# Attention scores of two heads on the two row halves of TensorE

## The chip, the cores and the metric

The kernel runs on one core of a Trainium2 chip. The metric is the device time of one execution in microseconds (us): the lower the better. The core has a matmul engine (TensorE, PE in the profile; its weight loads are a row of their own, PEld), a vector engine (DVE), an engine for activations (ACT), GpSimd (POOL) and SyncE (SP), which issues transfers. Each works through its own queue in order, and they wait for each other by semaphores. A matmul holds one operand, the weights, in the 128 x 128 array, and streams the other through it; the results land in PSUM, a memory of eight banks that hold 512 fp32 values in each of 128 partitions.

## The reference

One layer of a transformer: attention, then a mixture of experts, each between two norms. Cut to what matters:

```
x = x + LN(attention(LN(x)))          # x: 8 images of 256 rows, 256 wide
x = x + LN(experts(LN(x)))            # 8 experts, 2 chosen per row, and 2 shared ones

attention: q = rope(x Wq)             # 32 heads of 8
           k = rope(x Wk), v = x Wv   # 8 key heads of 8: four query heads share one
           scores = q k^T / sqrt(8)   # causal
           ctx = softmax(scores) v
           return ctx Wo + b
```

The whole is fp32. The attention has eight key heads, and for each of them four query heads, over 256 rows of each image.

## The kernel before

The kernel goes through the eight images (b = 0 to 7) in two row halves each (tt, 128 rows), and records every step with a due time by `at(when, step, ...)`; the steps are then issued sorted by these times, each onto all the engines it uses. So the due times alone, in units of one image, set the order in every queue: scores of one image are made beside the projections of the next and the shared experts of an earlier one. After the eight images come the routed experts (in blocks of 256 rows), the additions to the result and the last norm.

Scores in fp32 quality come from fp32r matmuls, which stream one column per step but keep fewer bits. So each head's eight values are split (`split`, POOL, and DVE for the first image's second half) into a rounded part and the rest; 32 rows hold the four combinations of both parts of q and k. Three key heads with 32 rows each, 96 rows (`SHIFT`), are one group; the eight heads make groups of three, three and two (`J`, `NS`, `heads_in`).

- `keysT` (L410) transposes the keys of a half by matmuls with an identity, three of them, 96, 96 and 64 columns of weights, and ACT or DVE copies the result to `kA`. `keys_apart` (L428) then moves it by three DMAs of SP into `kst`: one block of 256 columns per key head, in which only the 32 rows of that head are not zero. Thus a matmul over all 96 rows, whose other operand holds three heads, gives the scores of one head.
- `queriesT` (L437) transposes the queries: per half three groups of four matmuls, 96, 96 and 64 weight columns, each group copied by ACT to `qA` (L444).
- `maxima` (L468, L475, L482) computes scores with queries as weights, and up to 512 columns of several key heads. A second matmul (bf16, an identity as weights) adds the causal mask to the diagonal part, and DVE reduces to the negated maximum of each row. An image has 32 of these scores, each with its mask, in 26 banks.
- `split_shift` and `shiftT` (L500) split these maxima, transpose them and put them by three DMAs of SP into six further rows of `qA` (96 to 101). The same rows of `kst` hold ones for the head's own two of them (`place1`, `set_ones`), so that the next matmul subtracts the maximum.
- `weights_of` (L520, L528, L530) computes the scores again, transposed, over all 102 rows: one matmul of 512 columns for each key head and pair of row blocks. ACT makes the exp, and POOL clears the part above the diagonal.
- `values` (L548) multiplies four of these with the values: four matmuls on four strips of 32 columns of the array at once. `softmaxed` (L568) turns and divides.

All the scores, the shared experts' products (`gu`, `po`) and later the experts share five PSUM banks (`ps_mm`); transposes have two of their own (`ps_tp`). Operands that live longer are held three times over (`qAs`, `ksts`, by b % 3); they are cleared at their first use by `clear_operands`, on DVE for the first, on POOL for the others.

Of the kernel before, what the change touches and what calls it, by code (L numbers as in the profile page):

```python
# [9 lines left out]
F32 = mybir.dt.float32  # L10
# [8 lines left out]
P = 128  # L19
EPS = 1e-5  # L20
NEG = -1e30
HD = 8
HB = 32
SHIFT = 96
# [4 lines left out]
def attn_moe_kernel(  # L29
# [63 lines left out]
    J = 3  # L93
    NS = -(-NKV // J)
    KR = SHIFT + 2 * J
# [74 lines left out]

    place1 = aconst.tile([P, J, 1], F32, name="place1")
    nc.gpsimd.memset(place1[SHIFT:P], 1.0)
    for sign, base in ((1, 0), (-1, 1)):
        nc.gpsimd.affine_select(
            out=place1[SHIFT:P],
            in_=place1[SHIFT:P],
            pattern=[[-2 * sign, J], [0, 1]],
            compare_op=ALU.is_ge,
            fill=0.0,
            base=base,  # L180
            channel_multiplier=sign,
        )
    qAs, ksts, v_aug = {}, {}, {}

    def clear_operands(i):
        qAs[i] = aconst.tile([P, NS * G, T], F32R, name=f"qA_{i}")
        engine = nc.gpsimd if i > 0 else nc.vector
        engine.memset(qAs[i][:, (NS - 1) * G :, :].bitcast(F32), 0.0)
        t = ksts[i] = aconst.tile([P, NKV, T], F32R, name=f"kst_{i}")
        engine.memset(t[0:SHIFT].bitcast(F32), 0.0)  # L190

    def set_ones(i):
        t = ksts[i]
        for k0 in range(0, NKV, J):
            n = min(J, NKV - k0)
            nc.scalar.copy(
                t[SHIFT:P, k0 : k0 + n, :], place1[SHIFT:P, 0:n, :].to_broadcast([P - SHIFT, n, T])
            )
# [139 lines left out]
    def project(b, tt):  # L338
# [32 lines left out]
        qs = work.tile([P, NS * G, J * HB], F32R, tag="qs", name=f"qs{b}_{tt}")  # L371
        ks = work.tile([P, NKV * HB], F32R, tag="ks", name=f"ks{b}_{tt}")
        held["qs", b, tt] = full, qs, ks

    def split(b, tt, i):

        full, qs, ks = held["qs", b, tt]
        if i == 0:
            to = ks.rearrange("p (h b a d) -> p h b a d", b=2, a=2, d=HD)
            of = full[:, NH:, :].unsqueeze(2).to_broadcast([P, NKV, 2, HD])  # L380
            pairs = [(to[:, :, :, 0, :], to[:, :, :, 1, :], of)]
        else:
            c, b2 = divmod(i - 1, 2)
            n = heads_in(c)
            to = qs[:, ts(c, G), 0 : n * HB].rearrange(
                "p g (j a b d) -> p j g a b d", a=2, b=2, d=HD
            )
            of = full[:, c * J * G : (c * J + n) * G, :].rearrange(
                "p (j g) d -> p j g d", g=G
            )  # L390
            pairs = [(to[:, :, :, 0, b2, :], to[:, :, :, 1, b2, :], of)]
# [5 lines left out]
    def heads_in(c):  # L397
        return min(J, NKV - c * J)

    def keysT(b, tt):  # L400
        ks = held["qs", b, tt][2]
        if tt == 0:
            held["kA", b] = work.tile(
                [SHIFT, NS, T], F32R, tag="kA", name=f"kA{b}", bufs=1
            )
        kA = held["kA", b]
        pt = ps_tp.tile([P, NS, P], F32, tag="tp", name=f"pkT{b}_{tt}")
        for c in range(NS):
            n = heads_in(c) * HB
            nc.tensor.matmul(  # L410
                pt[0:n, c, :],
                lhsT=ks[:, c * SHIFT : c * SHIFT + n],
# [4 lines left out]
        whole = NKV // J  # L417
        copied = copier(b - 1)
        copied(kA[:, 0:whole, ts(tt, P)], pt[0:SHIFT, 0:whole, :])
        if whole < NS:  # L420
            copied(kA[0:n, whole, ts(tt, P)], pt[0:n, whole, :])

    def keys_apart(b):
        kA, kst = held.pop(("kA", b)), ksts[b % 3]
        for j in range(J):
            n = len(range(j, NKV, J))
            part = slice(HB * j, HB * j + HB)
            nc.sync.dma_start(  # L428
                out=kst[part, j:NKV:J, :].bitcast(F32), in_=kA[part, 0:n, :].bitcast(F32)
            )  # L430

    def queriesT(b, tt, c):
        qs = held["qs", b, tt][1]
        n = heads_in(c) * HB
        pt = ps_tp.tile([P, G, P], F32, tag="tp", name=f"pqT{b}_{tt}_{c}")
        for g in range(G):
            nc.tensor.matmul(  # L437
                pt[0:n, g, :],
                lhsT=qs[:, c * G + g, 0:n],
                rhs=ident_r,  # L440
                start=True,
                stop=True,
            )
        nc.scalar.copy(qAs[b % 3][0:n, ts(c, G), ts(tt, P)], pt[0:n])  # L444

    def maxima_of(b, tt):

        width = (tt + 1) * P
        for c in range(NS):
            per = min(512 // width, heads_in(c))  # L450
            for k0 in range(0, heads_in(c), per):
                nk = min(per, heads_in(c) - k0)
                ng = 512 // (nk * width)
                for g0 in range(0, G, ng):
                    yield c, c * J + k0, nk, g0, ng

    def maxima(b, tt, c, k0, nk, g0, ng):

        qA, kst = qAs[b % 3], ksts[b % 3]
        if ("nmx", b, tt) not in held:  # L460
            held["nmx", b, tt] = small.tile(
                [P, NKV, G], F32, tag="nmx", name=f"nmx{b}_{tt}", bufs=2
# [3 lines left out]
        sc = ps_mm.tile([P, ng, nk, width], F32, tag="mm", name="sc")  # L466
        for g in range(ng):
            nc.tensor.matmul(  # L468
                sc[:, g, :, :],
                lhsT=qA[0:SHIFT, c * G + g0 + g, ts(tt, P)],  # L470
# [835 lines left out]
```

## Time and profile before

| What | us |
|---|---|
| median of 6 runs (832.1 to 840.11) | 835.98 |
| the profiled execution | 841.12 |
| its span | 839.4 |
| PE busy, of the span | 774.6 (92%) |
| PEld busy | 589.7 (70%) |
| DVE busy | 421.7 (50%) |
| POOL busy | 344.5 (41%) |
| ACT busy | 259.9 (31%) |
| scores for the weights (L520), 192 matmuls | 97.2 |
| scores for the maxima (L468), 256 matmuls | 101.2 |
| mask (L475), 256 matmuls | 74.5 |
| values (L548), 384 rows of the profile | 58.2 |

A plain fp32 matmul stands as two rows in the profile, each of two passes; an fp32r, a bf16 one and a transpose stand as one. [...] A shape such as 96*128 means 96 rows and 128 weight columns. The tables' times count from the start of the span. The images take from about 20 us to about 515 us, and the routed experts the rest.

### The profile page before, as it was taken

Reading aid. Unit: us, or ns where it says so; the run is one execution under the profiler, and the core shown is the slowest. Engines: PE = TensorE matmul, PEld = TensorE weight load, DVE = VectorE, ACT = ScalarE, POOL = GpSimd, SP = SyncE. Lnnn points to the kernel's source line nnn. Section 1 sums busy time; section 2 is a strip of 40 time slices with the busy share of each in tenths; the row PEclk is TensorE's granted clock in tenths of the full one; section 3 lists DMA queues with packets and bytes.
Section 4 is the critical chain, followed back from the end, with each engine's and each line's share of the span. In section 5 each row is a group of like instructions: output and inputs, shape, how many; then the busy total and the mean of one; then the engine's idle time right before and its main releaser. Section 6 shows DMA issues by size and latency. Waiting matters only on the chain. (4 is left out here: it accounts for less than half of the span.)

```text
span 839.4 us, 11794 instructions
## 1 busy us (share of the span) xinstructions
PE 774.6 (92%) x4041; PEld 589.7 (70%) x4041; DVE 421.7 (50%) x1172; ACT 259.9 (31%) x567; POOL 344.5 (41%) x616
## 2 busy tenths in 40 slices
PE   5989899999999999999999987999999999999753
PEld 3545466767767767767756666888888888889742
DVE  5756677677677677676685446122222222222215
ACT  3554444234244234244234321112121111212103
POOL 4567445435435435434244422531213434252213
PEclk8799899999999999999999997999999999999986
DMA  5023300000000000000000005525556575779642
GB/s 151 6 83 87 87 16 16 7 21 15 7 22 15 7 22 16 13 15 15 21 8 2 27 0 201 184 55 196 156 164 211 146 226 149 212 201 338 223 114 100
DMA packets 31906, 74.62 MB, mean 89 GB/s; under 512 B 9136, under 2 KB 26032, under 8 KB 28896
## 3 DMA queue, kind: packets, MB, share of 16 engines
q1 hardware_dynamic: 20304, 58.17, 19.7%
q0 software_dynamic: 8224, 10.03, 7.1%
q10 hardware_dynamic: 3312, 5.60, 2.4%
q8 instruction: 35, 0.57, 0.3%
q14 instruction: 31, 0.25, 0.1%
HBM read 59.36 MB, written 11.80 MB: 85 GB/s over the span
## 5 line engine op out<-in xcount | busy, mean ns | idle before, releaser
L776 PE MATMUL gu<-xgT,w 128*128 128x256 f32 (+1 forms) x840 | 163.9, 354 | 0.6 <-issue 0.3
L776 PE MATMUL gu<-x2T,ws_sb 128*128 128x256 f32 x640 | 155.9, 391 | 5.2 <-PEq L1207 5.0
L776 PEld LDWEIGHTS gu<-xgT,w 128*128 128x128 f32 x840 | 144.4, 190 | 17.6 <-issue 0.5
L528 ACT ACTIVATE ex<-scT 128x512 f32<-128x512 f32 x192 | 113.6, 597 | 137.1 <-PE scT L520 124.8
L482 DVE TENSOR_REDUCE nmx<-sc 128x2 f32<-128x512 f32 (+2 forms) x208 | 129.2, 642 | 26.5 <-PE sc L475 26.2
L776 PEld LDWEIGHTS gu<-x2T,ws_sb 128*128 128x128 f32 x640 | 121.8, 196 | 27.5 <-issue 6.2
L530 POOL TENSOR_SCALAR_AFFINE_SELECT ex<-ex 128x512 f32<-128x512 f32 x128 | 81.1, 639 | 114.0 <-ACT ex L528 113.8
L979 DVE TENSOR_TENSOR act<-sg,gu 128x256 f32<-128x256 f32 (+1 forms) x105 | 40.9, 389 | 128.8 <-ACT sg L978 128.8
L468 PE MATMUL sc<-kst,qA 96*128 96x512 f32 (+2 forms) x256 | 101.2, 426 | 0.8 <-issue 0.5
L987 POOL DMA_INDIRECT sums<-yb,of x37 | 58.3, 1575 | 101.8 <-DVE yb L986 62.7
L520 PE MATMUL scT<-qA,kst 102*128 102x512 f32 x192 | 97.2, 514 | 1.8 <-DMA qA<-nm 1.8
L978 ACT ACTIVATE sg<-gu 128x256 f32<-128x256 f32 (+1 forms) x105 | 37.6, 358 | 190.1 <-PE gu L776 190.1
L789 PE MATMUL po<-ws_sb,sact 128*128 128x256 f32 x320 | 78.3, 403 | 13.8 <-DVE sact L806 9.5
L789 PEld LDWEIGHTS po<-ws_sb,sact 128*128 128x128 f32 x320 | 63.8, 203 | 28.8 <-DVE sact L806 9.9
L789 PE MATMUL po<-w,act 128*128 128x256 f32 x370 | 83.2, 379 | 0.0
L789 PEld LDWEIGHTS po<-w,act 128*128 128x128 f32 x370 | 68.8, 190 | 8.5
L475 PE MATMUL sc<-mask,ident_b 128*128 128x256 bf16 (+2 forms) x256 | 74.5, 294 | 0.0
L924 POOL DMA_INDIRECT xg<-rows,of x39 | 37.7, 967 | 87.1 <-DMA of<-slots 34.7
L811 DVE SCALAR_TENSOR_TENSOR th<-th,gu 128x256 f32<-128x256 f32 x70 | 29.3, 418 | 66.2 <-ACT th L810 66.2
L468 PEld LDWEIGHTS sc<-kst,qA 96*128 96x128 f32 x256 | 51.4, 201 | 13.7 <-issue 3.9
L548 PE MATMUL av<-ex,v_aug 128*32 128x512 f32 x384 | 58.2, 605 | 1.3 <-POOL ex L530 1.3
L810 ACT ACTIVATE th<-gu 128x256 f32<-128x256 f32 x70 | 26.8, 383 | 99.6 <-PE gu L776 98.1
(166 smaller groups left out, 845.2 us busy)
## 6 DMA issues: line engine op xcount, KB each, us to landing
w<-in_routed SPq DMA_DIRECT2D x23, 1920.0 KB
ws_sb<-in_shared ACTq DMA_DIRECT2D x8, 480.0 KB
xs<-in_x SPq DMA_DIRECT2D x8, 256.0 KB
rows<-x2n SPq DMA_DIRECT2D x8, 256.0 KB
acc<-sums SPq DMA_DIRECT2D x4, 512.0 KB
sums<-ya SPq DMA_DIRECT2D x14, 128.0 KB
kst<-kA SPq DMA_DIRECT2D x16, 96.0 KB
out<-acc SPq DMA_DIRECT2D x3, 512.0 KB
```

The costliest lines, as they stand in the source:

```text
L468: nc.tensor.matmul(sc[:, g, :, :], lhsT=qA[0:SHIFT, c * G + g0 + g, ts(tt, P)], rhs=kst[0:SHIFT, k0 : k0 + nk, 0:width], start=True, stop= ...
L475: nc.tensor.matmul(sc[:, g, :, width - P :], lhsT=ident_b, rhs=mask.unsqueeze(1).to_broadcast([P, nk, P]), start=False, stop=True,)
L482: nc.vector.tensor_reduce(nmx[:, k0 : k0 + nk, g0 : g0 + ng].rearrange("p k g -> p g k"), sc, AX.X, ALU.max, negate=True,)
L520: nc.tensor.matmul(sc, lhsT=ksts[b % 3][0:KR, kv, ts(s, P)], rhs=qAs[b % 3][0:KR, ts(kv // J, G), ts(t, P)], start=True, stop=True,)
L528: nc.scalar.activation(e, sc, AF.Exp, scale=QSCALE)
L530: nc.gpsimd.affine_select(out=e, in_=e, pattern=[[0, G], [1, P]], compare_op=ALU.is_ge, fill=0.0, base=0, channel_multiplier=-1,)
L548: nc.tensor.matmul(av[32 * j : 32 * j + 32, :], lhsT=v_aug[b % 3 * TT + s][:, c * G + j, :], rhs=e.rearrange("p g t -> p (g t)"), start=(s ...
L776: nc.tensor.matmul(gu[:, half, :], lhsT=m[:, k, ts(i, P)], rhs=xT[:, k, :], start=(k == 0), stop=(k == KC - 1),)
L789: nc.tensor.matmul(po, lhsT=act[:, k, ts(t, P)], rhs=d[:, k, :], start=(k == 0), stop=(k == ic - 1),)
L924: nc.gpsimd.indirect_dma_start(out=dst, out_offset=None, in_=src, in_offset=bass.IndirectOffsetOnAxis(ap=idx, axis=0),)
L979: nc.vector.tensor_tensor(act[:, i, :], sg, gu[:, 1, :], ALU.mult)
L987: put = nc.gpsimd.indirect_dma_start(out=sums, out_offset=bass.IndirectOffsetOnAxis(ap=of[:, t, 1:2], axis=0), in_=y, in_offset=None, comp ...
```

## The change

A group now holds two key heads, in rows 0 to 63 and 64 to 127 (`RB`): 32 rows of the head, two of zeros, two for the maximum, the rest unused. Four groups of two take the place of three of up to three. A matmul works on one head's half of the rows, and the two halves are issued one after the other, in pairs, into two banks.

The key operand needs no block of zeros any more: `keysT` makes four matmuls of 128 weight columns, whose copy goes straight to `kst`, and `keys_apart` with its DMAs goes, like `set_ones` and the clearing of `qA` and `kst`. The zeros and ones come with the untransposed keys and queries, which are now held once per half (`ks_of`, `qs_of`) and cleared at the start. `queriesT` makes four groups of four matmuls with 128 weight columns, and ACT copies all 128 rows. `maxima` makes per step the scores of two heads: eight matmuls of 128 columns in the first half (four steps), four of 256 in the second (eight steps), then two masks, one per bank, of 512 or 256 columns, and two reductions. `weights_of` makes two scores at once, in 36 rows each, and two exps. The maxima go to `qA` by two DMAs per half in place of three. Due times follow: steps of the maxima stand 0.07 apart in place of 0.032, those of the weights come two at a time at twice the distance, splits and query transposes stand a little closer, as there are more of them.

```diff
-SHIFT = 96
+RB = 64
+KS = HB + 2
+KR = KS + 2
...
-    J = 3
-    NS = -(-NKV // J)
-    KR = SHIFT + 2 * J
+    J = P // RB
+    NS = NKV // J
...
+    NQ = NH // 2 * HB
+    qs_of = [aconst.tile([P, NS // 2, NQ + HB], F32R, name=f"qs_{i}") for i in range(TT)]
+    ks_of = [aconst.tile([P, NS, J, RB], F32R, name=f"ks_{i}") for i in range(TT)]
...
     def clear_operands(i):
+        ks, qs = ks_of[i].bitcast(F32), qs_of[i].bitcast(F32)
+        nc.gpsimd.memset(ks[:, :, :, HB:], 0.0)
+        nc.gpsimd.memset(ks[:, :, :, KS:KR], 1.0)
+        nc.gpsimd.memset(qs[:, :, NQ:], 0.0)
...
     def keysT(b, tt):
...
+                pt[:, c, :],
+                lhsT=ks[:, c].rearrange("p j r -> p (j r)"),
...
+        copier(b - 1)(ksts[b % 3][:, :, ts(tt, P)], pt)
-    def keys_apart(b):
-        kA, kst = held.pop(("kA", b)), ksts[b % 3]
-        for j in range(J):
-            n = len(range(j, NKV, J))
-            part = slice(HB * j, HB * j + HB)
-            nc.sync.dma_start(
-                out=kst[part, j:NKV:J, :].bitcast(F32), in_=kA[part, 0:n, :].bitcast(F32)
-            )
...
     def queriesT(b, tt, c):
...
+            lo = (2 * J * g + c % 2) * HB
             nc.tensor.matmul(
-                pt[0:n, g, :],
-                lhsT=qs[:, c * G + g, 0:n],
+                pt[:, g, :],
+                lhsT=qs[:, c // 2, lo : lo + P],
...
+    def half_of(j, rows):
+        return slice(j * RB, j * RB + rows)
+    def maxima_of(tt):
+        ng = 512 // ((tt + 1) * P)
+        return [(c, g0, ng) for c in range(NS) for g0 in range(0, G, ng)]
...
+        sc = [ps_mm.tile([P, ng, width], F32, tag="mm", name="sc") for j in range(J)]
         for g in range(ng):
+            for j in range(J):
+                nc.tensor.matmul(
+                    sc[j][:, g, :],
+                    lhsT=qA[half_of(j, KS), c * G + g0 + g, ts(tt, P)],
+                    rhs=kst[half_of(j, KS), c, 0:width],
+                    start=(g == 0),
+                    stop=False,
+                )
+        for j in range(J):
             nc.tensor.matmul(
+                sc[j][:, :, width - P :],
                 lhsT=ident_b,
+                rhs=mask.unsqueeze(1).to_broadcast([P, ng, P]),
...
+            nc.vector.tensor_reduce(
+                nmx[:, j, c, g0 : g0 + ng], sc[j], AX.X, ALU.max, negate=True
+            )
...
+    def weights_of(b, c, s, t):
+        sc = [ps_mm.tile([P, G, P], F32, tag="mm", name="scT") for j in range(J)]
+        for j in range(J):
+            nc.tensor.matmul(
+                sc[j],
+                lhsT=ksts[b % 3][half_of(j, KR), c, ts(s, P)],
+                rhs=qAs[b % 3][half_of(j, KR), ts(c, G), ts(t, P)],
...
+        for j in range(J):
+            e = work.tile([P, G, P], F32, tag="ex", name="ex", bufs=EX)
+            nc.scalar.activation(e, sc[j], AF.Exp, scale=QSCALE)
...
-                when += 0.032
+                when += 0.07
...
-                for j in range(G):
-                    at(when, weights_of, b, c * G + j, s, t)
-                    when += unit
+                for j in range(0, G, J):
+                    at(when, weights_of, b, (c * G + j) // J, s, t)
+                    when += J * unit
```

## The prediction

> **What bounds the kernel now.** I read the busy shares by stage first, then the chain that ended last, then the timeline of TensorE, because that engine is what the stages agree on. The stage table (time from the span's start, then busy us of PE, PEld, DVE, ACT, POOL, then the granted clock) has this row for the attention stage:
>
> ```profile
> 60.00:480.00 420.00, 405.48 (x2259) 281.43 (x2257) 284.30 (x796) 162.13 (x338) 197.68 (x425) 0.99 0.08 22
> ```
>
> PE is busy 405 of 420 us (97%) at a granted clock of 0.99; the next engine, DVE, is at 68%, POOL at 47%, ACT at 39%. The chain that ended last shows only the tail (the additions into sums, then the last norm), which the change does not touch. So inside the stage a microsecond added to TensorE is a microsecond added to the end, and the other engines' additions are covered while they stay well under PE. What must be priced is therefore how long TensorE is *occupied*, start to next start, and not the durations printed for one matmul, which overlap. The timeline of PE alone gives that (start, duration, line, operation, shape, count):
>
> ```profile
> 232.32 0.45 PE L468 MATMUL sc<-kst,qA 96*128 96x512 f32 x1
> 232.61 0.28 PE L475 MATMUL sc<-mask,ident_b 128*128 128x256 bf16 x1
> 232.65 0.47 PE L520 MATMUL scT<-qA,kst 102*128 102x512 f32 x1
> 232.96 0.22 PE L500 MATMUL pm<-ident_r,nhl 128*64 128x128 f32 x1
> ...
> 235.21 1.06 PE L661 MATMUL pl<-wr_sb,x2T 128*128 128x8 f32 x8
> 236.12 0.48 PE L520 MATMUL scT<-qA,kst 102*128 102x512 f32 x1
> ...
> 239.34 0.28 PE L475 MATMUL sc<-mask,ident_b 128*128 128x256 bf16 x1
> 239.56 1.07 PE L548 MATMUL av<-ex,v_aug 128*32 128x512 f32 x8
> 240.55 1.56 PE L343 MATMUL pq<-wqkv,xnT 128*128 128x384 f32 x4
> 241.66 0.69 PE L468 MATMUL sc<-kst,qA 96*128 96x512 f32 x1
> 242.18 0.28 PE L475 MATMUL sc<-mask,ident_b 128*128 128x256 bf16 x1
> 242.30 1.89 PE L776 MATMUL gu<-x2T,ws_sb 128*128 128x256 f32 x8
> ...
> 249.13 0.36 PE L468 MATMUL sc<-kst,qA 96*128 96x256 f32 x1
> 249.34 0.23 PE L475 MATMUL sc<-mask,ident_b 128*128 128x128 bf16 x1
> 249.38 0.36 PE L468 MATMUL sc<-kst,qA 96*128 96x256 f32 x1
> ```
>
> Four things are to be seen. A score of 512 columns with its mask takes 0.33 us (232.32 to 232.65), one of 256 columns with its mask 0.25 (249.13 to 249.38). A matmul that streams almost nothing but loads 128 weight columns takes 0.91 / 8 = 0.114 us (235.21 to 236.12): that is the price of a weight load that nothing covers, and the floor of a matmul of 128 columns with 128 weight columns. The values (L548) run on four column strips at once: eight matmuls take 0.99 us (239.56 to 240.55), where the same in sequence would take eight times 0.43. So strips do run side by side. And a strip costs something at both ends: from mask to values 0.22 us, from the same mask to an ordinary matmul 0.12 (242.18 to 242.30), so 0.10 on the way in; and the first matmul after it finds its weights not loaded. For the latter compare the four pq matmuls above, 1.11 us to the next start, with the same four elsewhere, 0.99:
>
> ```profile
> 36.52 1.46 PE L343 MATMUL pq<-wqkv,xnT 128*128 128x384 f32 x4
> 37.51 0.69 PE L468 MATMUL sc<-kst,qA 96*128 96x512 f32 x1
> ```
>
> Last, two scores of the weights in a row, between matmuls of the same kind:
>
> ```profile
> 203.11 0.81 PE L520 MATMUL scT<-qA,kst 102*128 102x512 f32 x2
> 203.76 0.81 PE L776 MATMUL gu<-x2T,ws_sb 128*128 128x256 f32 x3
> ```
>
> They take 0.65 us, of which 0.19 belong to the matmul before (started 0.03 before the scores, though it needs 0.22): 0.23 each.
>
> **The change, part by part.** The prices above are at full clock. One image has two row halves; there are 8 images, 16 halves.
>
> *Transposes (L410, L437): more.* Their cost follows the weight columns loaded: mean loads of 128, 96 and 64 columns last 190, 163 and 136 ns (loads by shape, 250 to 400 us), 27 ns per 32 columns, and matmuls stand 85 ns apart with 96 columns and 60 with 64. Queries: 8 x 85 + 4 x 60 = 0.92 us per half become 16 x 112 = 1.79; keys: 2 x 84 + 60 = 0.23 become 4 x 112 = 0.45. +1.09 us per half, **+17.5**.
>
> *Scores of the weights (L520): less.* 192 x 0.23 = 44.2 us become 96 pairs of 0.23: **-22.1**, if halves of the rows overlap as the strips of L548 do.
>
> *Maxima (L468, L475): less.* Before, per image, 20 scores with mask of 768 columns together at 0.33 and 12 smaller ones at 0.245: 9.54 us. After: first half, 4 steps of four pairs (128 columns, load bound, 0.112) and two masks of 512 columns (0.23, twice the 0.12 row less its fixed part): 4 x 0.90; second half, 8 steps of two pairs (0.112) and two masks of 256 (0.12): 8 x 0.47. Together 7.36. 8 x (7.36 - 9.54) = **-17.4**. The columns of mask are as many as before.
>
> *Changes of shape: new.* In the built order of PE the values form 48 stretches, so 96 changes. In the changed program there are 174 stretches of 64-row matmuls and 48 of values, 24 times next to each other: 420 changes, 324 more. The nearest row is L548: 0.095 us of waiting (0.10 in; out, 0.99 less two passes of 0.43 and 0.04 of load and stagger leaves 0.09). 324 x 0.095 = **+30.8**. Besides, weights can't be loaded ahead over such a change: 159 entries from ordinary work x 0.107 (128 columns) = 17.0, 69 exits to ordinary matmuls x 0.105 = 7.2 (the 0.11 of pq), 96 exits to the bf16 mask x 0.015 (its load lasts 97 ns against 190) = 1.4, less 2.0 for first loads that I had in the maxima: **+23.6**.
>
> Sum: 17.5 - 22.1 - 17.4 + 30.8 + 23.6 = +32.4 us. Streaming saves 22.0, and changes at 0.168 each give back 54.4; the break-even is 22.0 / 324 = 0.068 us per change. The bounds of that price: the 64-column matmul of L500 (0.31 from L520 to it, as to any other, so 0.00) below, the 0.20 of L548 (0.095 and a full load) above. I take L548's, since it is the only row where strips alternate. With 0.00 for wait and load the sum is -22.0, with the wait gone and the loads exposed +1.6, with 0.20 throughout +42.8.
>
> [...]
>
> *Edits with no price, and their cover.* POOL's splits go from 14 to 18 instructions per half, at the first image's durations 4.45 to 5.15 us, +11 in all, covered by POOL's idle half. ACT: 16 more query copies of 0.58 (+9.3), less the 9 casts of ones (lots of three, 2.07), with one key copy of 512 columns for two (0.37 and 0.26), on an engine at 39%. DVE: 192 reductions of 512 (0.68) instead of 208 at 0.642, level; two memsets (0.91, 1.76) before its first rope go, and they were waited out anyway. SP: 24 key DMAs and 16 of the shift DMAs go; the first maxima waited longer for query copies (last at 21.1) than for the key DMA (issued 17.3). At the start two more copies (+1.2) stand against the casts gone (up to -2): 0 taken, -2 to +2 kept. If POOL's cover goes, its +0.7 per half lands on the transposes: 11 at most.
>
> *Two banks at a time.* Each pair takes two of the five score banks. What waits behind is every later matmul on PE, then exps. A bank is held for 0.60 (exp) or 0.68 (reduction); PE's waits for those are small now (1.7 for reductions). Bounds 0 and 96 x 0.68 / 4 = 16, if a quarter of the maxima steps wait a reduction; I take 0, as two reductions (1.36) fit in the 5.2 us per maxima step (62 per image / 12).
>
> Profiled time 841.1 (span 839.4) + 32.4 = 873.5; taking 2.4 off for the first 60 us, where PE is idle a quarter of the time and hides its share, 871. The median of the runs is 836.0, 5 below: **866**.
>
> **Rivals.** (A) The forecast, changes cost as at L548: 852 to 882 (0.045 to 0.11 of drain, start and small waits). (B) *Faster or level:* a half-array shape costs nothing to enter, as L500, and loads run ahead: -22, 814; with loads exposed 838; so 812 to 846. For it: L500's row. Against: 64 columns are used there by single matmuls, not alternating. It decides below 0.068 per change. (C) *The two halves don't overlap:* loads or matmuls go one after the other. Weights lose the 22.1, the maxima 14.3 in each half (4 or 2 more loads of 0.112 per step, 32 and 64 steps): +50.7 on top, 917; partly, from 885. For it: no row shows row strips; against: L548's loads start side by side (eight loads busy 0.16). (D) *Bank waits:* A + 16, 870 to 895, by the bound above.
>
> **How the numbers follow.** A 0.57, B 0.20, C 0.15, D 0.08. Below 836 lies some 0.14 of B, above 895 some 0.08 of C: 836 to 895. A alone is 852 to 882. A measurement tells about 0.5% (4 us) from no change: faster is below 832 (0.16, from B), within 0.5% 0.04, slower 0.80.
>
> **What would show it.** Pairs of L478 and L429 starting some 7 ns apart (else C); from the mask to such a pair 0.22 rather than 0.12, and a first matmul of 0.1 longer behind it (else B); queries' transposes 0.112 apart; PE's occupied time per image 62 to 66. Wrong would make it: a change under 0.07, a halved array that serves one matmul at a time, or exps and reductions that release banks late, seen as PE idle before L429 or L478.

## The result, and the profile after

The changed kernel takes 910.5 us (median; 903.9 to 918.4) against 836.4 us for the kernel before: 1.0885 times as long, 95% interval 1.0863 to 1.0907. The forecast was 866, and 910.5 lies above the upper end of its range, 895. The direction was right, the size was not: 74 us were added where 30 were expected.

The profiled execution has a span of 907.8 us. The first view is the one that the prediction began with, busy time by stretch (time from the span's start, then busy us of PE, PEld, DVE, ACT and POOL, the granted clock, the share of the DMA engines and GB/s), with two stretches in which the clock stands out:

```profile
60.00:480.00 420.00, 390.87 (x2154) 256.72 (x2155) 242.63 (x651) 144.48 (x308) 178.20 (x432) 0.90 0.06 18
20.00:75.00 55.00, 51.65 (x223) 32.32 (x223) 24.21 (x53) 18.60 (x36) 19.50 (x58) 0.56 0.10 28
75.00:180.00 105.00, 95.50 (x496) 58.32 (x494) 57.97 (x153) 39.31 (x81) 52.58 (x141) 0.80 0.12 36
```

The same two stretches of the kernel before:

```profile
20.00:75.00 55.00, 50.08 (x263) 29.48 (x263) 34.24 (x76) 31.08 (x60) 32.59 (x86) 0.88 0.20 53
75.00:180.00 105.00, 98.60 (x539) 65.45 (x537) 70.05 (x193) 42.01 (x87) 54.21 (x123) 0.97 0.13 37
```

PE is busy 93% of the stage from 60 to 480 us where it was 97%, and its clock there is 0.90 where it was 0.99. Between 20 and 75 us the clock is 0.56: most of that stretch ran at half speed. All the other engines are less busy than before, so none of them became the bound; TensorE itself got slower, and it waits.

The next view is PE's timeline in the middle of the stage (start, duration, line, operation, shape, count, and the idle time before it with what ended it):

```profile
299.58 1.99 PE L735 MATMUL gu<-x2T,ws_sb 128*128 128x256 f32 x8
301.50 0.51 PE L429 MATMUL sc<-kst,qA 34*128 34x256 f32 x4
301.94 0.39 PE L437 MATMUL sc<-mask,ident_b 128*128 128x256 bf16 x2
302.09 0.64 PE L386 MATMUL pkT<-ident_r,ks 128*128 128x128 f32 x4
302.66 0.49 PE L478 MATMUL scT<-qA,kst 36*128 36x512 f32 x2
303.09 0.65 PE L527 MATMUL pav<-ident,avs 128*128 128x128 f32 x4
...
307.80 1.11 PE L400 MATMUL pqT<-ident_r,qs 128*128 128x128 f32 x4 [4.06 <-POOL qs L380]
308.71 3.40 PE L735 MATMUL gu<-x2T,ws_sb 128*128 128x256 f32 x8
312.04 0.50 PE L429 MATMUL sc<-kst,qA 34*128 34x256 f32 x4
```

Two things are to be seen. First, the local prices of the prediction are about right. A step of the maxima, four scores of 256 columns in two pairs, takes 0.44 us up to its masks (301.50 to 301.94), where the prices make 0.33 (two pairs of 0.112 and the way out, 0.11); a pair of scores of the weights with its way out takes 0.43 (302.66 to 303.09), where they make 0.43 (0.23 and 0.20). The single records put the two matmuls of a pair at 301.505 and 301.508, and at 302.661 and 302.664: the two row halves do run side by side. Second, something is there that the prediction did not have. At 303.7 PE stops for 4.06 us, because the transposes of the queries wait for POOL's split. And then the same eight products of the shared experts that took 1.92 us to the next start (299.58 to 301.50) take 3.33 (308.71 to 312.04). The clock by stretch says why:

```profile
297.70:303.70 6.00, 6.00 (x40) 3.44 (x36) 5.72 (x19) 2.11 (x5) 4.07 (x10) 1.00 0.01 1
303.70:307.80 4.10, 0.04 (x2) 0.00 (x1) 1.47 (x4) 0.63 (x2) 3.33 (x9) 0.64 0.02 1
307.80:311.60 3.80, 3.80 (x11) 3.26 (x12) 0.00 (x0) 0.58 (x1) 1.94 (x8) 0.50 0.00 0
311.60:320.00 8.40, 8.40 (x50) 5.65 (x50) 5.10 (x15) 4.27 (x10) 1.74 (x3) 1.00 0.01 2
```

The clock is granted in full until PE stands still (1.00), and at half for the work that follows the wait (0.50 from 307.8 to 311.6 us). Such waits come once in an image; the chart of PE's waits has them first (us in total, times, longest):

```profile
PE pqT L400 <- POOL qs L380: 18.1, 8, 4.4
```

POOL's timeline shows what it was doing meanwhile:

```profile
298.17 0.24 POOL L379 CAST qs<-full 128x64 fp32r<-128x64 f32 x1
298.48 0.32 POOL L380 TENSOR_TENSOR qs<-full,qs 128x64 fp32r<-128x64 f32 x1
...
300.37 1.08 POOL L709 DMA_INDIRECT slots<-records,to  x1 [0.53 <-POOL records L703]
...
301.96 0.98 POOL L709 DMA_INDIRECT slots<-records,to  x1 [0.28 <-POOL records L703]
302.95 0.24 POOL L379 CAST qs<-full 128x64 fp32r<-128x64 f32 x1
303.28 0.31 POOL L380 TENSOR_TENSOR qs<-full,qs 128x64 fp32r<-128x64 f32 x1
...
304.02 1.00 POOL L709 DMA_INDIRECT slots<-records,to  x1 [0.28 <-POOL records L703]
...
305.53 0.98 POOL L709 DMA_INDIRECT slots<-records,to  x1 [0.28 <-POOL records L703]
306.53 0.24 POOL L379 CAST qs<-full 128x64 fp32r<-128x64 f32 x1
306.86 0.31 POOL L380 TENSOR_TENSOR qs<-full,qs 128x64 fp32r<-128x64 f32 x1
307.12 0.23 POOL L379 CAST qs<-full 128x64 fp32r<-128x64 f32 x1
307.43 0.32 POOL L380 TENSOR_TENSOR qs<-full,qs 128x64 fp32r<-128x64 f32 x1
```

The splits of the queries stand in POOL's queue between the scatters of the router (`scatter`, L703 and L709, about 1.5 us apart, from an earlier image). The changed layout packs two groups of queries beside each other, and a transpose of 128 weight columns for one group reads parts of the other. So the first group now waits for the splits of two groups, with scatters between them: its own two (298.17 and 302.95) are done at 303.59, before PE stops, and the second group's two (306.53 and 307.12) at 307.75, just before PE goes on.

**Where the 74 us are.** I took the time up to the block table (512.2 us before, 586.4 after) apart for each image: PE idle; PE busy while the clock record says half, of which half is counted as lost (as if all of it took twice as long, which is an assumption); and the rest, the work at full clock. Idle time is counted from PE's first matmul; the 7 us before it are in the sum of the last column.

| Part | before | after | more | PE idle | lost to half clock | work at full clock |
|---|---|---|---|---|---|---|
| first four images | 148.6 | 185.5 | 36.9 | +2.0 | +34.7 | +0.3 |
| next three | 185.9 | 215.2 | 29.3 | +10.9 | +10.9 | +7.5 |
| from there to the block table | 177.8 | 185.7 | 7.9 | +5.1 | +1.6 | +1.1 |
| sum | 512.2 | 586.4 | 74.2 | +17.9 | +47.3 | +8.9 |

The parts after the table take 327.2 us before and 321.4 after; the difference is mostly one wait of an expert for its activation, which is 9.5 us in one profile and 3.5 in the other, and which is long or short in the experiments' profiles too, whichever kernel it is. Of 74 us, 47 are the clock, 18 are waits, and only 9 are what the prediction had calculated. A second profile of the changed kernel, the control below, gives 39, 22 and 11 of 72: it has 16 us less at half clock, all of it in the first four images.

### The profile page after: what moved, and what is told of

Its sections match the earlier page's. It is cut to its first block, busy times and chain, and to the rows that moved or that the text cites. A ratio compares the mean times of both kernels' runs of the same rounds, so it can differ in the third digit from the quotient of the medians.

```text
span 907.8 us, 12263 instructions
## 1 busy us (share of the span) xinstructions
PE 829.6 (91%) x4313; PEld 610.5 (67%) x4313; DVE 417.1 (46%) x1148; ACT 257.1 (28%) x568; POOL 348.5 (38%) x675
## 5 line engine op out<-in xcount | busy, mean ns | idle before, releaser
L735 PE MATMUL gu<-x2T,ws_sb 128*128 128x256 f32 x640 | 171.1, 419 | 6.8 <-PEq L1164 5.4
L735 PEld LDWEIGHTS gu<-x2T,ws_sb 128*128 128x128 f32 x640 | 130.1, 211 | 36.6 <-issue 7.3
L444 DVE TENSOR_REDUCE nmx<-sc 128x2 f32<-128x512 f32 (+1 forms) x192 | 122.7, 682 | 43.1 <-PE sc L437 43.0
L487 ACT ACTIVATE ex<-scT 128x512 f32<-128x512 f32 x192 | 104.3, 595 | 113.7 <-PE scT L478 110.7
L489 POOL TENSOR_SCALAR_AFFINE_SELECT ex<-ex 128x512 f32<-128x512 f32 x128 | 78.7, 639 | 132.6 <-ACT ex L487 132.6
L400 PE MATMUL pqT<-ident_r,qs 128*128 128x128 f32 x256 | 52.0, 344 | 19.7 <-POOL qs L380 18.1
L400 PEld LDWEIGHTS pqT<-ident_r,qs 128*128 128x128 f32 x256 | 43.9, 245 | 34.1 <-POOL qs L380 21.3
L429 PEld LDWEIGHTS sc<-kst,qA 34*128 34x128 f32 x512 | 42.7, 209 | 28.5 <-issue 20.0
L429 PE MATMUL sc<-kst,qA 34*128 34x256 f32 (+1 forms) x512 | 59.1, 328 | 1.8 <-DVE cum L242 0.8
L507 PE MATMUL av<-ex,v_aug 128*32 128x512 f32 x384 | 60.3, 651 | 0.5 <-POOL ex L489 0.5
```

What stands on the lines that cost most here:

```text
L400: nc.tensor.matmul(pt[:, g, :], lhsT=qs[:, c // 2, lo : lo + P], rhs=ident_r, start=True, stop=True,)
L429: nc.tensor.matmul(sc[j][:, g, :], lhsT=qA[half_of(j, KS), c * G + g0 + g, ts(tt, P)], rhs=kst[half_of(j, KS), c, 0:width], start=(g == 0) ...
L444: nc.vector.tensor_reduce(nmx[:, j, c, g0 : g0 + ng], sc[j], AX.X, ALU.max, negate=True)
L487: nc.scalar.activation(e, sc[j], AF.Exp, scale=QSCALE)
L489: nc.gpsimd.affine_select(out=e, in_=e, pattern=[[0, G], [1, P]], compare_op=ALU.is_ge, fill=0.0, base=0, channel_multiplier=-1,)
L507: nc.tensor.matmul(av[32 * j : 32 * j + 32, :], lhsT=v_aug[b % 3 * TT + s][:, c * G + j, :], rhs=e.rearrange("p g t -> p (g t)"), start=(s ...
```

## The experiments

Thirteen kernels were run. The theory to be tested has three parts: (1) the waits come from POOL's order, and each brings a spell of half clock behind it; (2) the other spells come because matmuls of 34 or 36 rows use a small part of the array, so that the clock is halved though TensorE is busy; (3) the changes of shape cost time of their own, of about the predicted size. The main rivals are that the waits alone explain the loss, that only the time in which TensorE streams counts for the clock, and that other engines bind the first images. In the expectations of the first runs part (2) still stands as the rival 'rows', against a clock theory that counts streaming time; its 3.4 us are the shortest spell of half clock in the clock record of the changed kernel's profile (3.41 us), and that a stretch of this length decides was an assumption. The run with 64 rows turned that round.

The changed kernel was run once more beside some of the others, as the control.

> The changed kernel unaltered, beside the next three on one chip: 904 to 916, half-clock time of the attention 115 to 150 us. If it comes out near 901, the 9 us by which the run with 64 rows was faster were a difference between chips.

It took 917.9 us against 844.2 for the kernel before on that chip, 1.0868 (1.0843 to 1.0892). The ratio repeats. Up to the block table this profile has 46.9 us idle (43.2 in the first) and 107.4 us busy at half clock, below the 115 to 150 expected and 16 less than the 123.3 of the first. So a difference of that size between two profiles tells nothing alone, and the granted clock of all the runs is given beside it where it matters. In the three middle images the two profiles agree (21.9 us at half clock in both).

### The scatters later

```diff
-            at(a + 0.39 + 0.03 * t, scatter, b, t)
+            at(a + 0.49 + 0.03 * t, scatter, b, t)
```

> The changed kernel with one due time moved: the router's scatter steps of POOL 0.1 image later, so that the splits of the next queries do not stand behind them. Clock theory (the granted clock halves after a stretch of about 3.4 us in which TensorE streams little, whether it waits or changes shape): the waits of L400 for the splits (17 us in five images) go and so do the half-clock spells right behind them (about 8 us of loss); the spells in stretches of many shape changes stay: 910 - 25 = 885. Rival 'waits only' (only waits of PE halve the clock): all later spells go too, 873. Rival 'rows' (the clock counts active rows of the array): only the waits go, 893.

It took 892.2 us, 1.0652 (1.061 to 1.0694): 18 us less than the changed kernel. That is the number of the rival that counts rows (893), not the 885 of the theory as it then stood, nor the 873 of the rival in which only waits halve the clock. PE's waits now have:

```profile
PE pqT L400 <- POOL qs L380: 3.1, 3, 2.0
```

18.1 us of waiting have become 3.1. Idle time fell by 13.0 us (16.7 against the control's profile). So the cause of the waits is the order of POOL's queue. What half clock went with them can be read in the three middle images alone: 21.9 us became 13.6. So spells remain there without such waits. But 55 us of the loss stay, and in the view by stretch the clock of the first images has hardly moved:

```profile
20.00:75.00 55.00, 49.20 (x221) 30.87 (x221) 23.95 (x52) 18.24 (x36) 19.50 (x58) 0.59 0.09 26
75.00:180.00 105.00, 100.03 (x539) 61.11 (x538) 62.99 (x165) 41.87 (x87) 53.96 (x143) 0.83 0.13 38
```

### The wait filled

From the fourth image on, twenty bf16 matmuls of 384 columns with an identity as weights, whose results are overwritten, stand where the wait is; POOL's order is not touched.

```diff
+        if tt == 1 and c == 0 and b >= 3:
+            fill(pt, 20)
         for g in range(G):
```

> The changed kernel with 20 extra matmuls of the bf16 identity (384 columns each, 3.2 us in all) in front of the query transposes that wait for POOL's splits in five images; they write the bank that the transposes then overwrite, and fill the wait without ending it. Cell theory (the granted clock halves after a stretch of 3.4 us in which the array's cells, rows times weight columns times streamed columns, are used below about 0.30 of their full rate, and returns above about 0.36; worked out from the ten traces so far): the waits stay, the half-clock spells of 6.8 us behind them go, 3.4 us each: -10 to -17, ratio to before 1.068 to 1.076 instead of 1.088. Rival (the spells are set by the 64-row shape, or by the wait on POOL itself): no change, 1.085 to 1.090.

It took 901.2 us, 1.0795 (1.0743 to 1.0846): less gain than the 1.068 to 1.076 expected, more than the none of the rival. The view by stretch right behind one filling (297.3 to 300.7 us), where the changed kernel had the spell:

```profile
300.00:320.00 20.00, 20.00 (x123) 13.72 (x122) 10.89 (x28) 8.86 (x19) 7.30 (x18) 1.00 0.01 2
```

The clock is full throughout; in the changed kernel it was at half for 6.8 us there. An image takes 68.6 us in place of 71.9: idle fell from 5.0 to 1.9, time busy at half clock from 7.3 to 0, and work rose from 63.4 to 66.6, which is the filling. The transposes still have to wait for POOL, and what was idle is filled by work of the same length; the 3.3 us gained are the clock's. This tells the wait and the spell apart: about half the cost of such a wait comes after it.

### How many rows a score uses

Four kernels change only the rows that the scores read. The first reads all 64 rows of each half. The added rows of the keys hold zeros, and in the maxima also two rows of ones, which shift all scores of a query alike.

```diff
-                    lhsT=qA[half_of(j, KS), c * G + g0 + g, ts(tt, P)],
-                    rhs=kst[half_of(j, KS), c, 0:width],
+                    lhsT=qA[half_of(j, RB), c * G + g0 + g, ts(tt, P)],
+                    rhs=kst[half_of(j, RB), c, 0:width],
...
-                lhsT=ksts[b % 3][half_of(j, KR), c, ts(s, P)],
-                rhs=qAs[b % 3][half_of(j, KR), ts(c, G), ts(t, P)],
+                lhsT=ksts[b % 3][half_of(j, RB), c, ts(s, P)],
+                rhs=qAs[b % 3][half_of(j, RB), ts(c, G), ts(t, P)],
```

> The changed kernel with 64 rows in each half's matmul instead of 34 and 36; the added rows of the keys are zeros and ones, which shift the maxima by a constant for each query. Same shapes, order and columns, twice the active rows. Clock theory (share of time streaming): no change, 907 to 914, the half-clock time of the attention within 10 us of the 133 of the changed kernel. Rival 'rows': most of the spells outside the waits go, 880 or less.

It took 901.0 us, 1.0778 (1.0739 to 1.0817), where a theory that counts streaming alone has no change to offer: not one matmul, column or wait of the program is different. The view by stretch of this kernel:

```profile
20.00:75.00 55.00, 48.22 (x227) 30.94 (x227) 25.33 (x55) 18.74 (x36) 19.43 (x58) 0.66 0.10 26
75.00:180.00 105.00, 94.74 (x539) 58.78 (x538) 63.13 (x165) 41.91 (x87) 53.77 (x143) 0.89 0.13 38
```

The same of the control:

```profile
20.00:75.00 55.00, 49.80 (x223) 31.92 (x224) 23.86 (x52) 18.70 (x36) 19.42 (x58) 0.57 0.07 20
75.00:180.00 105.00, 93.36 (x512) 57.41 (x511) 61.13 (x158) 39.88 (x83) 52.56 (x141) 0.85 0.14 41
```

0.56 (0.57 in the control) became 0.66, and 0.80 (0.85) became 0.89; the time busy at half clock fell from 123.3 (107.4) to 89.5 us. The granted clock of the four runs is 0.929 to 0.932, that of the changed kernel's 25 runs 0.904 to 0.929. In this kernel the rows that a matmul has active count for the clock. The gain is smaller than that theory had put it (880 us or less).

The next three let the scores read rows 0 to 97 as one whole, at full height; that undoes the pairs and the changes of shape, and keeps the order and the number of matmuls. Their scores are those of both heads added up: in the first everywhere, in the second only for the maxima, in the third only for the weights.

```diff
-                    lhsT=qA[half_of(j, KS), c * G + g0 + g, ts(tt, P)],
-                    rhs=kst[half_of(j, KS), c, 0:width],
+                    lhsT=qA[0 : RB + KS, c * G + g0 + g, ts(tt, P)],
+                    rhs=kst[0 : RB + KS, c, 0:width],
...
-                lhsT=ksts[b % 3][half_of(j, KR), c, ts(s, P)],
-                rhs=qAs[b % 3][half_of(j, KR), ts(c, G), ts(t, P)],
+                lhsT=ksts[b % 3][0 : RB + KS, c, ts(s, P)],
+                rhs=qAs[b % 3][0 : RB + KS, ts(c, G), ts(t, P)],
```

> The changed kernel with the scores' matmuls over rows 0 to 97 instead of one half each, so none has the 64-row shape; each then sums the scores of both heads, and the attention is that of the sum, not the reference's. Pairs, transposes, POOL's order stay. Clock theory: streaming +39 us, shape changes -54 by my prices, and the spells outside the waits go back to those of before, -35: about 860, the spells behind the waits of L400 stay. Rival 'waits only': the waits stay, so the spells stay, 910 - 15 = 895. Rival 'rows': 98 rows active, spells go, also 860 (the run with 64 rows tells this one apart).

> The changed kernel with the maxima's matmuls alone over rows 0 to 97 (they see the sum of both heads' scores, so the subtracted value is not the maximum), the weights' scores in 64-row pairs. By my prices the 64-row shape is level in the maxima (saves 3.5 us an image in streaming, costs 3.7 in changes), so the occupied time stays; by the run with full rows it saves 10 us in all, so 0 to 10 more here. Clock theory: in the maxima each pair of steps has two changes of shape in 0.8 us, so most of the early half-clock spells are theirs and go: 890 to 898. Rival: the spells belong to the weights' pairs, 910.

> The changed kernel with the weights' scores alone over rows 0 to 97 (both heads' scores are summed there), the maxima in 64-row steps. By my prices the pairs lose 1.7 us an image against full rows, so the occupied time falls by 13 and the time to 895; by the run with full rows, where the 64-row shape saved 10 us in all, it rises by up to 10. Clock theory: the maxima's spells stay, 897 to 912. Rival (spells belong to the weights' pairs): 885 to 890.

The times of the first (899.6 us) and of the others (921.4 and 904.2) are from two chips, so they are compared by ratio; the other columns are from the profiles, in us up to the block table.

| Scores in full height | ratio | PE idle | busy at half clock | work at full clock | clock, 20 to 75 us |
|---|---|---|---|---|---|
| none (the control) | 1.0868 (1.0843 to 1.0892) | 46.9 | 107.4 | 483.5 | 0.57 |
| maxima and weights | 1.0774 (1.0727 to 1.082) | 49.8 | 73.3 | 491.5 | 0.76 |
| maxima | 1.0888 (1.0854 to 1.0922) | 47.6 | 97.6 | 495.0 | 0.69 |
| weights | 1.0702 (1.0678 to 1.0725) | 47.0 | 88.0 | 485.3 | 0.64 |

The columns of half clock and of work must be read apart. In the three middle images, where little runs at half clock, the work is 189.9 us with the row halves, and 190.3, 193.0 and 189.1 in full height (both, maxima, weights). So in all the halves are level with full height in the same order: overlapping streams give about what the changes of shape take. They gain 1.0 us an image in the maxima and lose 0.3 in the weights. The 8.0 us that the halves save in the column of work (491.5 less 483.5) lie for the most part in the first four images (6.5), where the count depends on how half clock is charged.

And the halves cost clock: 34 us more at half speed, 17 lost. The granted clock of the runs agrees: 0.933 to 0.939 with all scores in full height, 0.904 to 0.929 in the changed kernel. Yet of the first four images 45.7 us remain at half clock (75.6 in the control, 22.0 in the kernel before), which the rows of the scores do not explain.

The expected times were missed. For the first kernel 860 stood against 899.6, since the changes of shape did not cost 15 us more than the overlap gives, and the spells went only in part. For the maxima 890 to 898 stood against a ratio that is the control's, and my expectation that the spells belong to them fell: undoing them took 10 us of half-clock time away, undoing the weights' pairs 19. Which of the two has the greater part is not shown, as two profiles of one kernel differ by 16 and the granted clocks of the runs lie together (0.922 to 0.929 and 0.926 to 0.930; the control on that chip 0.907 to 0.918).

### Fewer changes of shape

From the second image on, steps of the maxima get the due times of the scores of the weights, so that they stand next to each other and share one change.

```diff
-        when = b - 0.98
+        when = b - 1 + 1e-4 if b > 0 else b - 0.98
...
-                when += 0.07
+                when += 2 * 0.98 / 24 if b > 0 else 0.07
```

> The changed kernel with the maxima of the next image due right behind a pair of the weights (not for the first image), so that 64-row stretches merge: 312 changes of shape instead of 420, everything else the same. At 0.09 to 0.168 us a change: -10 to -18, and some spells fewer, -5: ratio 1.060 to 1.075. Rival (four of the five banks held at a time): PE waits in front of the maxima eat it, 1.085 or more.

It took 898.9 us, 1.0758 (1.0716 to 1.08). Counted in the order of PE's matmuls, 420 changes have become 313. The work fell from 481.5 to 466.0 us, 0.145 for each change; in one of the middle images from 63.4 to 60.6 with 16 fewer of 54, 0.175 each. The prediction had 0.168. Idle time rose from 43.2 to 57.0, nearly as much as the work fell, most of it the wait for POOL's splits (18.1 us became 26.3). So much of the gain in work went into waits. The time at half clock is 99.1 us, where the two profiles of the changed kernel have 123.3 and 107.4, and the granted clock of the runs (0.914 to 0.926) is not apart from the changed kernel's: that the clock gained is not shown.

### The cures together

The first of these has the later scatters, the 64 rows, and the merged steps from the first image on; there the second half of the first image is scored before its maxima have arrived, and subtracts other values. The second merges only from the second image on, as above.

> The changed kernel with three cures: the router's scatter 0.1 image later, 64 rows per matmul, and the maxima of the next image due right behind a pair of the weights, which merges 64-row stretches (312 changes of shape instead of 420). Clock theory: -18 from the waits as measured, -9 from the rows as measured, 108 changes at 0.09 to 0.168 us = -10 to -18, and fewer spells, -5: 860 to 868. Rival (four of the five banks taken at a time): PE waits in front of the maxima, 880 or more. Either way above 837, since the transposes (+17) stay.

> The changed kernel with the three cures (router's scatter later, 64 rows, merged stretches from the second image on). As the run with all three, whose second half of the first image was scored before its maxima had arrived: ratio 1.035 to 1.045. What is left should be the half clock of the first 120 us (25 us by the trace of that run), while the steady images take 62 to 64 us as before the change.

The first took 879.1 us, 1.0407 (1.0385 to 1.043), the second 864.7 us, 1.0335 (1.0295 to 1.0375): with three small edits 54% and 62% of the loss are gone. The first stayed behind its 860 to 868, the second came out a little better than its 1.035 to 1.045. Two of the three middle images of the second take 62.1 us, as in the kernel before (62.1), without half clock. Yet nothing is gained there, and the first four images still take 171.0 in place of 148.6 us. Of these 22 us, 18.5 are time lost to half clock (59.0 us busy at half clock, against 22.1) and 3.9 are idle; the work is level (124.1, 124.0). The view by stretch of the second:

```profile
20.00:75.00 55.00, 48.33 (x230) 31.31 (x230) 25.44 (x56) 19.09 (x37) 19.46 (x58) 0.65 0.10 25
75.00:180.00 105.00, 96.27 (x576) 63.01 (x575) 67.14 (x173) 43.69 (x90) 58.18 (x156) 0.90 0.13 39
```

To see whether that rest can be had, the second was run with extra matmuls of the identity in the first four images: five before the transposes of the keys and two before each group of the queries' in the first image (the first line), and up to two in each step of the maxima (the last).

```diff
+        if b == 0:
+            fill(pt, 5)
...
+        fill(sc[0], 2 if b <= 1 else 1 if b <= 3 else 0)
```

> The three cures together (scatter later, 64 rows in the scores, maxima and weights merged), and besides extra bf16 matmuls of an identity: five before each key transpose group and two before each query group of the first image, two before each step of the maxima for the first two images, one for the third and fourth. Their results are overwritten. The kernel with the cures alone took 864.7 us (ratio 1.0335); its images from 171 us on are level with before, and all it still loses, 22 us, lies in the first 171 us, where TensorE is busy 59 us at half the clock. Theory (the clock follows how much of the array works in a window): with the array kept in use there, the half-clock time falls by most of the 29 us that it costs, less what the extra matmuls occupy at full clock: 15 to 25 us less, ratio 1.005 to 1.018. Rival: the first 171 us are bound by query copies, reductions and splits, and the low clock is only what TensorE shows while it waits: ratio 1.03 or more.

It took 869.2 us, 1.0416 (1.0343 to 1.049): no better than without, and far from the 1.005 to 1.018 of the theory. That is the rival's number, but its first stretch is not the rival's picture:

```profile
20.00:75.00 55.00, 48.61 (x289) 27.63 (x289) 28.31 (x62) 19.36 (x39) 22.28 (x63) 0.88 0.10 29
```

The clock rose from 0.65 to 0.88, and PE did not wait more: idle in the first four images fell from 17.4 to 13.2 us, and busy time at half clock from 59.0 to 37.0, which saves 11. But the work rose by 19 us, so the sum is 4 us longer: that is the fillings themselves, and the changes of shape that they bring back, since a filling stands between the 64-row stretches that had been merged (377 changes in the order of PE's matmuls, 313 without). PE stands still for 13 of these 175 us, so other engines do not bind these images; and this filling is no way to gain there; I had put what it occupies too low. No kernel was run that keeps the array in use there without extra work.

### The kernel before, with one idea of the change

The change writes one mask over a whole bank. The kernel before can do that too, with its three heads in 96 rows; the second kernel below adds the fillings of the first image.

```diff
-                start=True,
+                start=(g == 0),
                 stop=False,
             )
-            nc.tensor.matmul(
-                sc[:, g, :, width - P :],
-                lhsT=ident_b,
-                rhs=mask.unsqueeze(1).to_broadcast([P, nk, P]),
+        nc.tensor.matmul(
+            sc.rearrange("p g k w -> p (g k) w")[:, :, width - P :],
+            lhsT=ident_b,
+            rhs=mask.unsqueeze(1).to_broadcast([P, ng * nk, P]),
...
```

> The kernel before with one part of the change alone: one mask matmul for each bank of maxima instead of one behind each score (26 masks an image for 32). By the start-to-start rows of before, two times 0.245 become two scores at 0.12 and a mask of 256 columns at 0.12 in four banks an image: -0.12 us each, and about -0.03 in two more: -0.55 us an image, 4 us in all, 832 against 836. Rival: the mask's own cost is hidden behind the next weight load, 836.

> The kernel before with one mask matmul per bank (0.9969 by itself) and extra matmuls of the bf16 identity in the first image alone: 5 of 384 columns in front of each half's key transposes, 2 in front of each group of query transposes, into the banks that these then overwrite. Cell theory: the spell from 16.0 to 29.7 us, in which TensorE is busy 7 us and more at half clock, does not start: -3 to -5 us, ratio 0.991 to 0.994. Rival (the copies of ACT and the splits of POOL bound that stretch): 0.997.

The first took 834.4 us, 0.9969 (0.995 to 0.9988): the fastest of all, by 0.3%. That is less than the 4 us expected and less than the 0.5% that I called measurable, but its interval leaves 1 out. Its stage up to the block table shortened from 512.2 to 509.9 us. The second took 835.8 us, 0.9991 (0.9959 to 1.0022), where 0.991 to 0.994 was expected. Its profile shows the effect on the clock that was meant; the row of its first stretch is shown for the kernel with one mask, and then for the one with the fillings besides:

```profile
15.00:30.00 15.00, 12.12 (x49) 7.95 (x49) 9.85 (x31) 9.20 (x18) 9.15 (x22) 0.66 0.07 18
```

```profile
15.00:30.00 15.00, 11.59 (x75) 7.96 (x73) 10.09 (x33) 9.75 (x20) 10.48 (x26) 1.00 0.08 20
```

The spell of half clock at the start is gone, and the stage is 508.0 us long, 1.9 less; over whole executions that cannot be told from nothing.

## Why the prediction was right and wrong

**Right: the direction and its reason.** TensorE was the bound, the two halves overlap (rival C is out: pairs start 3 ns apart), transposes stand 0.114 us apart where 0.112 was priced, a change of shape costs (rival B is out: it would have needed less than 0.068, and taking 107 changes away gave 0.145 each), and banks were no trouble (rival D: PE waits 0.6 us for the reductions before L429, and 1.4 for exps before the `gu` matmuls, where 16 was the bound). This reason alone made 9 to 20 of the 74 us. What a change of shape consists of, the "drain, start and small waits" of the prediction, no run shows apart; the 0.145 is for the whole.

**Too large: the sum of the work.** It was +32.4 us (some 30 with what the first 60 us were to hide). The work at full clock rose by 8.9 us in the sum, or by 2.5 an image in the middle ones, which makes 20 in eight; the prices make 4.05 an image. The runs in full height part this. By the prices the halves save 50.7 us against full height in the same order (the loss of rival C) and their changes cost 54.4, so the halves lose 0.5 us an image; measured, they gain 0.1. That term was 0.6 too high; as the price of a change held (0.145 to 0.175 for 0.168), the overlap gave somewhat more than was priced. The other 1.0 lies in the new order at full height, 2.6 an image more than before where the prices make 3.6. As the transposes held, it is left to the maxima and their masks; that is by difference, and no run measures it alone. This error alone would have made the forecast too high, not too low.

**Failed step 1: "covered by POOL's idle half".** The prediction priced the splits' own time, +0.7 us per half, 11 at most, and looked for cover in POOL's mean share. POOL is not busier than before (47% of the stretch from 60 to 480 us, then 42%). What it missed is order: the first group of queries needs the splits of two groups, and in POOL's queue scatters stand between them. Moving the scatters alone took 13.0 us of idle time away, and 18 us of the median. The number of instructions was priced; which of them the first reader waits for was not.

**Failed step 2: "The prices above are at full clock".** The granted clock was read once, as 0.99, and taken as a property of the stage. It goes with what TensorE does: filling the wait took an image's time at half clock from 7.3 us to 0, and 64 rows took the clock between 20 and 75 us from 0.56 to 0.66. 47.3 of the 74.2 us are time lost at half clock (39 in the control's profile). The kernel before shows it too: its clock is 0.88 between 20 and 75 us. The allowance of 2.4 us for the first 60 us had the wrong sign: in the first four images, the part that was to hide a share of the change, half of the loss arose. There the shared experts' products, which use the whole array, are not running yet (the profile has none of the `gu` matmuls until 140 us; before the change they begin at 113), and matmuls of 34 and 36 rows are much of what TensorE has: 92 of its 223 between 20 and 75 us. That the rows count is shown by the run with 64 of them. They are not all of it: in full height 45.7 us stay at half clock in the first four images, against 22.0 before the change, and where these come from stays open. No rival contained the clock, so the upper end of the range, made from bank waits and a part of rival C, stood on mechanisms that did not happen; 910 lay only within C's own bounds, and for another reason than C's.

## What to carry to other kernels

When a change makes matmuls smaller, count what part of the array they keep in use, stage by stage, and not only how long they take: here TensorE was busy 94% of the time between 20 and 75 us, at a clock of 0.56 where it was 0.88 before the change, and 64 rows in place of 34 and 36 brought 0.66. Look for stalls by order and not by share: ask which instructions the first reader now needs, and what stands between them in that queue; a wait of 4 us on the bound engine cost about as much again in what came after.

## What the runs showed of the hardware that was not expected

The clock record of both profiles, before and after the change, has two values, 1.00 and 0.50. In that of the changed kernel the spells of half clock inside the span last 3.41, 6.83, 10.24, 13.65, 17.07 and 30.72 us, multiples of the shortest. TensorE was busy 91% of this span, and the clock still cost 39 to 47 us more than before, some 5% of the span.

I counted from the matmul records of these two profiles, for each stretch of 3.41 us along the changes of the clock record, rows times weight columns times streamed columns, as a share of the whole array streaming without a break (256 columns twice in 0.216 us, the spacing of the `gu` matmuls). Of 440 stretches at full clock, the 29 with half clock behind them have shares of 0 to 0.37, the other 411 of 0.31 and more; of 62 at half clock, the 35 with half clock behind them have 0 to 0.37, the other 27 have 0.24 to 0.51. By streaming time alone it is 0 to 0.46 against 0.36 and more, and 0 to 0.83 against 0.68 and more. The ranges overlap in both counts, and no run was made to measure where the clock changes; the 0.30 and 0.36 that were expected of the filled wait are the author's fit to such counts. It is the run with 64 rows, in which nothing but the rows differs, that decides for the rows (a clock of 0.66 between 20 and 75 us, against 0.56 and 0.57).

Two matmuls on the two row halves start 3 to 4 ns apart (94 of the 96 pairs of L478 whose two records follow each other) where one score of 512 columns took 0.23 us, and so stream side by side in fp32r. A change of shape between them and the full array costs 0.145 to 0.175 us in this mixture, the exposed weight load included, so that the halves gain nothing clear over full height here (189.9 against 190.3 us in three images).
